# Two states' scan terms added on GpSimd before TensorE turns them

## The chip, the core and the metric

The kernel runs on one core of one Trainium2 chip. It is one program for the whole model of two layers, in float32 throughout (some operands of the attention are float32 rounded for TensorE). The metric is device time in microseconds (us) of the whole program; the times of a kernel are given as the median of several runs, and one further execution is profiled. Engines are named as the profile names them: PE is TensorE's matmul (PEld its weight load), DVE is VectorE, ACT is ScalarE, POOL is GpSimd, SP the queue that issues most DMAs.

## The reference, cut to what matters

The input is 4 images of 128 channels and 64 x 64 places. Layer 0 is a convolution branch with a Mamba scan over the 4096 places of an image; layer 1 is attention over the 4096 places (4 heads of 32) and a mixture of 8 experts, two chosen for each place. The change is inside the scan:

```python
dA = jnp.exp(delta[..., None] * A)
dBu = delta[..., None] * Bm[:, :, None, :] * xin[..., None]

def step(h, inp):
    dA_t, dBu_t, C_t = inp
    h = dA_t * h + dBu_t
    y = jnp.einsum('bdn,bn->bd', h, C_t)
    return (h, y)
...
y = jnp.transpose(ys, (1, 0, 2)) + D_skip * xin
out = y * jax.nn.silu(z) @ out_proj_w.T
```

There are N = 16 states for each of 64 inner channels and each of 4 groups of 32 channels. So y at a place is the sum over 16 states of state times C.

## The kernel before, in words

**Tiling.** An image of 4096 places is cut into NB = 8 blocks of BLK = 512; with 4 images there are 32 blocks. A block's scan has two parts p (two channel groups each, so that 2 x 64 channels fill 128 partitions), and each part has 16 states, taken in pairs. A pair is a *unit* (b, i, p, n) (line 1299): 16 units to a block, 512 in all. A unit takes two *slots* of the main loop (line 1322), an even and an odd one, so a block has 32 slots and the scan has END = 1024.

**A unit's work.** `driven` (799) multiplies the pair's rows of B, fetched by a DMA and the same for all channels, by delta times input into the tile `h` (DVE, 128x1024). `scan` (804) runs the recurrence through both states in one DVE instruction over 1025 elements, with decays `da` that ACT made (`decayed`, 779). In the odd slot `read` (813) multiplies h by the pair's rows of C into `hc`, 128 partitions x 2 states x 512 (DVE, two buffers). `kept` (794) stores the last column of each state for the next block.

**The sum over states** is made on PE: `turned_on` (824) transposes a term of 128x512 in four matmuls of 128x128 that accumulate into one PSUM tile `y`: 16 terms, one for each state, over the 8 units of a part. When a part's last term is in, ACT copies y out as yT, one slot later `turned_back` (839) transposes it back into another tile of the same PSUM pool, and a slot after that `summed_up` (833) lets DVE gate it.

**The order of work** is written out by hand. Every instruction of the main loop goes through `queued` (450), which fixes each engine's order to the order in which the program writes the instructions (so the profile gives one line, L467, for nearly all of them, and tiles tell them apart). In a slot the loop writes: the DMAs for rows to come, the next unit's decays, `driven` (even slot), what is left of a part that was closed, half a step of lane X, the scores and exponentials of one attention group, `scan` (even) or `read` (odd), half a step of lane Y, the terms that are due, the other half of lane Y, the products of the attention group before, the other half of lane X. Lane Y carries the convolutions, norms and inputs of the scan's next blocks; lane X the closing of blocks behind it and the experts. Each lane has one PSUM tile. Norms in both lanes raise a variance to the power -0.5 on POOL (tiles rsX, rsY, 128x4), which ACT (xt) or DVE (tt) then reads.

**When terms are due.** A deque `due` holds (slot, unit, which state, term, whether it ends the part), and the loop takes from its front whatever has come due (lines 1348 to 1359). A unit read in odd slot s has its first term due at s + 1 and its second at s + 2; the first unit of a part has its first term due at s + 3, and as the deque is taken from the front its second follows then too, so that y of the part before has left PSUM.

**Attention** groups (PE scores sc, ACT exponentials pT, PE products av) are ready only when their blocks are closed; they lag behind the scan and run on after its last unit.

Of the kernel before, what the change touches and what calls it, by code (L numbers as in the profile page):

```python
# [24 lines left out]
NST = 16  # L25
# [11 lines left out]
def conv_mamba_attn_moe_kernel(ctx: ExitStack, tc: tile.TileContext, t: dict):  # L37
# [3 lines left out]
    NB = L // BLK  # L41
# [419 lines left out]
    class Queue:  # L461
# [7 lines left out]
    tensor, vector, scalar, gpsimd, sync = (  # L469
        Queue(e) for e in (nc.tensor, nc.vector, nc.scalar, nc.gpsimd, nc.sync)  # L470
    )
# [14 lines left out]
    def flush():  # L486
        for entry in outgoing:
            entry[0] -= 1
            if entry[0] == 0:
                sync.dma_start(out=entry[1], in_=entry[2])  # L490
        outgoing[:] = [entry for entry in outgoing if entry[0]]
# [302 lines left out]
    def kept(unit, h):  # L794
        b, i, p, n = unit
        if i < NB - 1:
            scalar.copy(states[b % 2][:, p, n : n + 2], h[:, :, BLK - 1])

    def driven(unit, h, w):
        b, i, p, n = unit  # L800
        du = in_of[b, i, p][3]
        vector.tensor_mul(h[:, :, 0:BLK], w, du[:, None, :].to_broadcast([P, 2, BLK]))

    def scan(unit, h, da):

        b, i, p, n = unit
        h, da = (a.rearrange("p k q -> p (k q)")[:, 0 : 2 * BLK + 1] for a in (h, da))
        vector.tensor_tensor_scan(
            out=h, data0=da, data1=h, initial=states[b % 2][:, p, n : n + 1],
            op0=ALU.mult, op1=ALU.add,  # L810
        )

    def read(h, w):
        hc = mix.tile([P, 2, BLK], F32, name="hc", bufs=2)
        vector.tensor_mul(hc, w, h[:, :, 0:BLK])
        return hc
# [7 lines left out]
    def turned_on(y, term, first, last):  # L824

        for j in range(NT):
            s = slice(j * P, (j + 1) * P)
            tensor.matmul(
                y[:, s], lhsT=term[:, s], rhs=ident, start=first and j == 0,
                stop=last and j == NT - 1, is_transpose=True,  # L830
            )

    def summed_up(b, i, p, y):
        scanned(b, i, p, y)
        done.add(("scan", b, i, p))
        if p == 1:
            lanes["X"].appendleft((("closed", b, i), closed(b, i), []))

    def turned_back(b, i, p, yT):
        y = ps_y.tile([P, BLK], F32, name="y")  # L840
        for j in range(NT):
            tensor.transpose(y[:, j * P : (j + 1) * P], yT[:, j * P : (j + 1) * P], ident)
        return b, i, p, y
# [184 lines left out]
    def exponentials(group):  # L1028
        pTs = []
        for v, sc in group[3]:  # L1030
            pT = att.tile([P, 2, BLK], F32, name="pT", bufs=4)
            scalar.activation(pT, sc, AF.Exp, scale=ATT_SCALE)
            pTs.append((v, pT))
        return *group[:3], pTs, *group[4:]

    def weighted(group):
        b, q, h, pTs, first, last, prev, final = group
        if first:
            sums[0] = ps_av.tile([P, BLK], F32, name="av")
        av = sums[0]  # L1040
        for k, (v, pT) in enumerate(pTs):
            for u in range(2):
                mm(
                    av[64 * u : 64 * u + 2 * DH, :], v, pT[:, u, :],
                    first and k == 0, last and k == STEP - 1,
                )
        if last:
            avs = att.tile([P, BLK], F32, name="avs", bufs=2)
            if prev is None:
                scalar.copy(avs, av)  # L1050
            else:
                vector.tensor_add(avs, av, prev)


            if not final:
                partial[b, q, h] = dram.tile([P, BLK], F32, name=f"avd{q}{h}")
                send(partial[b, q, h], avs, 3)
                return
            if h == 0:
                total[b, q] = dram.tile([2, 2, NH, DH, BLK], F32, name=f"total{q}")  # L1060
            d = total[b, q]
            send(d[:, :, h].rearrange("u k r q -> (u k) r q"), avs, 3)
            if h == NH - 1:
                work_left = inverted(b, q)
                later.extend((slot + n, work_left) for n in (4, 6, 8))
# [150 lines left out]
    def advance(lane, second):  # L1216

        if inside[lane] != second:
            return False
        while True:  # L1220
            if lane not in running:

                tasks = lanes[lane] if lanes[lane] or slot < END else lanes["X"]
                if tasks and lane == "Y" and tasks[0][0][0] == "closed":
                    return False
                if not tasks or not all(k in done for k in tasks[0][2]):
                    return False

                if (
                    tasks[0][0][0] == "out" and slot < END + 4  # L1230
                    and not 2 <= slot % (2 * NST) < NST + 2
                ):
                    return False
                key, stages, _ = tasks.popleft()
                running[lane] = key, stages(lane) if callable(stages) else stages
            key, stages = running[lane]
            try:
                next(stages)
                inside[lane] = not second
                return True  # L1240
            except StopIteration:
                assert not second
                done.add(key)
                del running[lane]
# [53 lines left out]
    groups = attention_groups()  # L1298
    units = [(b, i, p, n) for b, i in blocks for p in range(2) for n in range(0, NST, 2)]
    END = 2 * len(units)  # L1300

    rows, due, closing, y_of = {}, deque(), deque(), {}
    h_of, slot = {}, 0

    def fetch(*wanted):
        for ahead, k in wanted:
            if ahead < len(units):
                until(("in", *units[ahead][:3]))
                rows[ahead, k] = fetched(units[ahead], k)

    def prepared(ahead, k):
        if ahead < len(units):
            decayed(units[ahead], decays[ahead % 2], k)
            if k:
                h_of[ahead] = carried(units[ahead])

    def ends(unit):
        return unit[3] == NST - 2
# [3 lines left out]
    while (  # L1322
        slot < END or due or closing or summing or waiting or left or later or lanes["X"] or running
    ):
        at, odd = divmod(slot, 2)
        flush()
        if slot == 0:
            fetch((0, 0), (0, 1), (1, 0))
            prepared(0, 0)
            prepared(0, 1)  # L1330
        fetch((at + 2, 0) if odd else (at + 1, 1))
        unit = units[at] if at < len(units) else None
        prepared(at + 1, odd)
        if unit and not odd:
            h = h_of.pop(at)
            driven(unit, h, rows.pop((at, 0)))
        if summing:
            summed_up(*summing)
            summing = None
        advance("X", True)  # L1340
        group = next(groups, None)
        if group:
            group = exponentials(group)
        if unit and not odd:
            scan(unit, h, decays[at % 2])
        if unit and odd:
            hc = read(h, rows.pop((at, 1)))
            late = 2 * (unit[3] == 0)
            due.append((slot + 1 + late, unit, 0, hc[:, 0, :], False))
            due.append((slot + 2, unit, 1, hc[:, 1, :], ends(unit)))  # L1350
        advance("Y", False)
        while closing and closing[0][0] <= slot:
            summing = turned_back(*closing.popleft()[1:])
        while due and due[0][0] <= slot:
            _, (b, i, p, n), k, term, done_with = due.popleft()
            first = n == 0 and k == 0
            if first:
                y_of[b, i, p] = ps_y.tile([P, BLK], F32, name="y")
            turned_on(y_of[b, i, p], term, first, done_with)
            if done_with:  # L1360
                yT = mix.tile([P, BLK], F32, name="yT")
                scalar.copy(yT, y_of.pop((b, i, p)))
                closing.append((slot + 1, b, i, p, yT))
        advance("Y", True)
        if unit and odd:
            kept(unit, h)
        if waiting:
            weighted(waiting)
        waiting = group
        advance("X", False)  # L1370
        while later and later[0][0] <= slot:
            next(later.popleft()[1])
        slot += 1
# [113 lines left out]
```

## Time and profile before

| what | value |
|---|---|
| median of 3 runs | 5234.72 us (5234.31 to 5243.44) |
| the profiled execution | 5221.24 us |
| its span, first to last instruction | 5219.4 us |
| first scan, first scan of the third block (slot 64), last scan start at | 99.4, 307.4, 4605.9 us |
| mean granted TensorE clock | 0.958 |

The page's strip of 40 equal slices shows how the load runs over the span. Each digit is the busy share of a slice in tenths, and PEclk is the granted clock in tenths of full speed:

```profile
PE   4566898999999999899999999999999999999997
PEld 2333444444444444444444444444444444443443
DVE  4888767777788877888788877888788877751332
ACT  3456787788777777688887787788777787756543
POOL 1111101100000000001000000000000001000000
PEclk8677999999999999899999999999999999999998
```

In the first four slices (some 520 us) little attention is ready and PE has gaps; from there to about slice 35 scan, lanes and attention run together; the last four or five slices are attention and experts without a scan. Rows of the page read: line, engine, operation, output tile <- input tiles, shapes, count | busy us of the group, mean ns of one | idle time of the engine before them and what ended most of it. Busy time is a union, so that overlapping matmuls count once, while the mean is the length of one record.

### The profile page before, as it was taken

The numbers are of one execution on the slowest core, as the hardware profiler recorded it, in microseconds if no ns is written. First come the engines' busy times: TensorE is split into PE (matmuls) and PEld (weight loads), VectorE is DVE, ScalarE is ACT, GpSimd is POOL, SyncE is SP. The second block draws the span as 40 slices with busy tenths as digits, with TensorE's granted clock in tenths as the row PEclk, the third lists the DMA queues.
The fourth block names the chain that finished last, engine by engine and source line by source line (L and its number), as shares of the span: only waits on it lengthen the run. The fifth ranks groups of instructions, "written<-read, shape, count | busy, mean of one in ns | idle before, by whom it ended". The sixth has DMA issues, their size and how long they took to land.

```text
span 5219.4 us, 62693 instructions
## 1 busy us (share of the span) xinstructions
PE 4743.5 (91%) x20704; PEld 2300.7 (44%) x20704; DVE 3834.5 (73%) x5809; ACT 3749.8 (72%) x5701; POOL 423.5 (8%) x483
## 2 busy tenths in 40 slices
PE   4566898999999999899999999999999999999997
PEld 2333444444444444444444444444444444443443
DVE  4888767777788877888788877888788877751332
ACT  3456787788777777688887787788777787756543
POOL 1111101100000000001000000000000001000000
PEclk8677999999999999899999999999999999999998
DMA  3556667767776667767766667767766666754542
GB/s 96 188 186 202 206 215 247 232 231 238 244 231 218 227 227 243 238 232 246 260 230 231 224 223 230 262 227 259 259 236 227 215 230 226 263 181 153 184 134 72
DMA packets 451694, 1131.62 MB, mean 217 GB/s; under 512 B 51985, under 2 KB 135330, under 8 KB 451362
## 3 DMA queue, kind: packets, MB, share of 16 engines
q1 hardware_dynamic: 450194, 1126.74, 64.3%
q8 instruction: 166, 2.72, 0.2%
q14 instruction: 166, 1.36, 0.1%
q10 hardware_dynamic: 1168, 0.80, 0.1%
HBM read 967.12 MB, written 143.39 MB: 213 GB/s over the span
## 4 chain that ended last, share of the span: by engine, by line
PE 55%; DVE 18%; ACT 13%; DMA 6%; issue 5%; POOL 2%; SPq 1%; DVEq 0%; ACTq 0%; POOLq 0%
PE av L467 23%; PE sc L467 13%; PE ps_X L467 8%; DVE h L467 6%; PE ps_Y L467 5%; PE y L467 5%; ACT pT L467 4%; ACT L467 3%; DMA ks<-kd 2%; DVE hc L467 2%; ACT xt L467 1%; ACT e L467 1%; DMA rows<-bcd 1%; DVE stX L467 1%; POOL rsX L467 1%
## 5 line engine op out<-in xcount | busy, mean ns | idle before, releaser
L467 ACT ACTIVATE pT<-sc 128x1024 f32<-128x1024 f32 x2048 | 1984.8, 1023 | 940.1 <-PE sc L467 938.4
L467 PE MATMUL av<-pT,v 128*64 128x512 f32 x8192 | 1998.3, 609 | 12.4 <-DVE avs L467 12.4
L467 PE MATMUL sc<-qs,ks 128*128 128x512 f32 x4096 | 1296.1, 436 | 64.4 <-DMA ks<-kd 32.7
L467 DVE TENSOR_TENSOR_SCAN h<-da,state,h 128x1025 f32<-128x1025 f32 x512 | 1204.2, 2352 | 90.0 <-ACT h L467 56.2
L467 PEld LDWEIGHTS sc<-qs,ks 128*128 128x128 f32 x4096 | 701.3, 190 | 793.3 <-ACT pT L467 261.7
L467 PEld LDWEIGHTS av<-pT,v 128*64 128x64 f32 x8192 | 499.5, 137 | 844.4 <-issue 813.8
L467 ACT ACTIVATE da<-delta,amat 128x512 f32<-128x512 f32 x1024 | 743.0, 730 | 1.9
L467 PE MATMUL y<-ident,hc 128*128 128x128 f32 x4096 | 626.6, 284 | 64.9 <-DVE hc L467 64.9
L467 DVE TENSOR_TENSOR hc<-rows,h 128x1024 f32<-128x1024 f32 x512 | 624.2, 1219 | 16.1 <-PE y L467 5.9
L467 DVE TENSOR_TENSOR h<-rows,du 128x1024 f32<-128x1024 f32 x512 | 623.4, 1218 | 14.2 <-DMA rows<-bcd 13.7
L467 PEld LDWEIGHTS y<-ident,hc 128*128 128x128 f32 x4096 | 520.6, 147 | 235.7 <-issue 83.9
L467 ACT ACT_TABLE_LOAD x319 | 409.3, 1283 | 19.5 <-DVE zs L467 14.3
L467 POOL TENSOR_TENSOR rsX<-rsX,mhalf 128x4 f32<-128x4 f32 x92 | 203.8, 2216 | 2524.6 <-DVE rsX L467 2440.5
L467 POOL TENSOR_TENSOR rsY<-rsY,mhalf 128x4 f32<-128x4 f32 x100 | 130.4, 1304 | 2071.0 <-DVE shiftY L467 1560.3
L467 DVE TENSOR_TENSOR avs<-av,prev 128x512 f32<-128x512 f32 x96 | 66.1, 689 | 252.9 <-PE av L467 238.3
L467 PE MATMUL ps_X<-share,w_ew 128*128 128x512 f32 x432 | 215.5, 622 | 8.7 <-DVE share L467 8.5
L467 ACT ACTIVATE xt<-ps_Y,shiftY,rsY 128x128 f32<-128x128 f32 x380 | 143.8, 469 | 106.4 <-POOL shiftY L467 99.0
L467 DVE TENSOR_TENSOR share<-share,xf 128x1024 f32<-128x1024 f32 x128 | 155.9, 1218 | 15.6 <-DMA share<-sharesX 9.9
L467 ACT COPY state<-h 128x2 f32<-128x2 f32 x448 | 88.7, 198 | 93.5 <-DVE h L467 93.5
L467 DVE SCALAR_TENSOR_TENSOR cm<-y,w_fc1w,cm 128x512 f32<-128x512 f32 x192 | 142.8, 744 | 3.4
L467 PE MATMUL ps_Y<-pairs,inxc 128*128 128x512 f32 x256 | 129.2, 629 | 15.6 <-DMA pairs<-xn 10.3
L467 PEld LDWEIGHTS ps_X<-share,w_ew 128*128 128x128 f32 x432 | 73.6, 190 | 146.8 <-issue 98.5
(254 smaller groups left out, 3455.8 us busy)
## 6 DMA issues: line engine op xcount, KB each, us to landing
rows<-bcd SPq DMA_DIRECT2D x1024, 512.0 KB
ks<-kd SPq DMA_DIRECT2D x192, 512.0 KB
qs<-qd SPq DMA_DIRECT2D x161, 512.0 KB
share<-sharesX SPq DMA_DIRECT2D x108, 512.0 KB
v<-vd SPq DMA_DIRECT2D x192, 256.0 KB
ks<-kd SPq DMA_DIRECT2D x128, 256.0 KB
avd<-avs SPq DMA_DIRECT2D x96, 256.0 KB
prev<-avd SPq DMA_DIRECT2D x96, 256.0 KB
```

What stands on the lines that cost most here:

```text
L467: return lambda *args, **kw: queued(op(*args, **kw))
```

## The change

From slot 64 on (ALONE = NB // 2 * NST = 4 x 16) the two terms of a unit are not turned one by one. In the odd slot, straight after `read`, GpSimd adds the second state's half of hc into the first, and PE gets one term of 128x512 to turn in place of two. That term is due at s + 2, or at s + 3 for the first unit of a part, and carries the mark that ends the part. Nothing else is edited.

```diff
@@ -1298,6 +1298,7 @@
     groups = attention_groups()
     units = [(b, i, p, n) for b, i in blocks for p in range(2) for n in range(0, NST, 2)]
     END = 2 * len(units)
+    ALONE = NB // 2 * NST
 
     rows, due, closing, y_of = {}, deque(), deque(), {}
     h_of, slot = {}, 0
@@ -1346,8 +1347,12 @@
         if unit and odd:
             hc = read(h, rows.pop((at, 1)))
             late = 2 * (unit[3] == 0)
-            due.append((slot + 1 + late, unit, 0, hc[:, 0, :], False))
-            due.append((slot + 2, unit, 1, hc[:, 1, :], ends(unit)))
+            if slot < ALONE:
+                due.append((slot + 1 + late, unit, 0, hc[:, 0, :], False))
+                due.append((slot + 2, unit, 1, hc[:, 1, :], ends(unit)))
+            else:
+                gpsimd.tensor_add(hc[:, 0, :], hc[:, 0, :], hc[:, 1, :])
+                due.append((slot + 2 + late // 2, unit, 0, hc[:, 0, :], ends(unit)))
         advance("Y", False)
         while closing and closing[0][0] <= slot:
             summing = turned_back(*closing.popleft()[1:])
```

## The prediction, made before the result was known

> **What bounds the kernel now.** I read the page's table of engines first, then the windows by block, then the chain.
>
> ```profile
> PE 4743.5 (91%) x20704; PEld 2300.7 (44%) x20704; DVE 3834.5 (73%) x5809; ACT 3749.8 (72%) x5701; POOL 423.5 (8%) x483
> ```
>
> PE leads, but a share of the span mixes stages. The windows that follow are five single blocks (16 units each) and the stretch after the last scan; after the length they give busy us of PE, PEld, DVE, ACT and POOL, then the granted clock.
>
> ```profile
> 307.40:426.20 118.80, 75.04 (x282) 41.63 (x281) 98.42 (x126) 63.81 (x120) 13.07 (x13) 0.77 0.55 186
> 551.20:682.50 131.30, 111.23 (x472) 55.47 (x470) 98.52 (x126) 93.99 (x155) 13.06 (x13) 0.91 0.61 205
> ...
> 1401.00:1541.00 140.00, 136.20 (x618) 66.27 (x615) 117.77 (x178) 112.54 (x175) 11.61 (x14) 1.00 0.69 226
> ...
> 1687.00:1830.00 143.00, 128.68 (x578) 64.89 (x576) 118.25 (x178) 108.91 (x174) 11.61 (x14) 0.95 0.69 237
> 1830.00:1974.00 144.00, 140.45 (x630) 68.75 (x627) 117.25 (x176) 115.86 (x180) 11.69 (x15) 0.99 0.69 226
> ...
> 4612.00:5219.40 607.40, 564.22 (x2229) 240.75 (x2228) 168.29 (x464) 300.56 (x334) 12.61 (x13) 0.96 0.41 135
> ```
>
> A regular block (1830 to 1974) takes 9.0 us a unit: PE is busy 97.5% of it (8.8 us a unit), DVE 81% (7.3 us). Where attention has not set in (307 to 426), neither is full. The last 607 us hold no scan and are out of the change's reach. Cut at each scan's start, the same block is uneven:
>
> ```profile
> 1834.60:1847.60 13.00, 13.00 (x54) 5.74 (x52) 6.68 (x7) 11.55 (x17) 0.00 (x0) 1.00 0.89 273
> 1847.60:1862.20 14.60, 14.60 (x78) 7.75 (x77) 9.69 (x19) 14.51 (x21) 1.91 (x1) 1.00 0.35 115
> ...
> 1886.70:1897.00 10.30, 10.30 (x47) 4.89 (x47) 10.23 (x11) 7.58 (x12) 0.00 (x0) 1.00 0.77 259
> ...
> 1964.50:1969.40 4.90, 4.90 (x25) 2.15 (x25) 4.71 (x4) 4.09 (x7) 0.00 (x0) 1.00 0.80 248
> ```
>
> DVE waits for PE in the first two and then has no gap at all. Cut so from 307 us on, DVE is over 90% busy in 226 of 479 stretches. The chain over those scans (307.4 to 4612, 4305 us) says which of the two counts:
>
> ```profile
> by line: PE av L467 22.3%; PE sc L467 12.7%; PE ps_X L467 8.4%; DVE h L467 6.5%; PE y L467 5.9%; ACT pT L467 5.1%; issue 5.0%; PE ps_Y L467 4.1%; ACT L467 3.8%; DMA ks<-kd 2.1%; DVE hc L467 1.9%; ACT xt L467 1.2%; ACT e L467 1.1%; DMA rows<
> ```
>
> So the chain goes from PE to DVE and back; y's transposes are on it for 5.9%, the scan's own DVE work (h and hc) for 8.4%.
>
> **What is removed: transposes on PE.** The rows of the page:
>
> ```profile
> L467 DVE TENSOR_TENSOR_SCAN h<-da,state,h 128x1025 f32<-128x1025 f32 x512 | 1204.2, 2352 | 90.0 <-ACT h L467 56.2
> ...
> L467 PE MATMUL y<-ident,hc 128*128 128x128 f32 x4096 | 626.6, 284 | 64.9 <-DVE hc L467 64.9
> ...
> L467 DVE TENSOR_TENSOR hc<-rows,h 128x1024 f32<-128x1024 f32 x512 | 624.2, 1219 | 16.1 <-PE y L467 5.9
> L467 DVE TENSOR_TENSOR h<-rows,du 128x1024 f32<-128x1024 f32 x512 | 623.4, 1218 | 14.2 <-DMA rows<-bcd 13.7
> ```
>
> The switch is at slot 64, and a block has 32 slots: it takes effect from the third block on, in 480 of 512 units (the instruction order of the built kernel agrees: 2176 such transposes are left and 480 adds stand on POOL). Four transposes a unit go, 1920 in all, at 626.6/4096 = 0.153 us of PE time each (their 284 ns overlap): 294 us of busy PE. Only what is on the chain pays. PE y there is 5.9% of 4305 = 254 us; yT's transposes are 40 us of the 667 us with that name, so hc's part is 239 us, and half of it, **-119 us**, goes. That is the most that this edit can bring while the rest of that chain stays. The first term was due a slot ahead of the second; now both come at the later slot, which already released y and yT, so nothing after it moves. The 65 us that PE waited for hc may shrink with that; it is counted as nothing, since 72 of the 78 hc on the chain are followed there by DVE's next instruction and not by PE.
>
> **What is added: 480 adds of 128x512 on POOL.** No such add is in the trace. The nearest rows are a copy and small products:
>
> ```profile
> 2318.36 0.20 POOL L467 TENSOR_TENSOR shiftY<-shiftY,rsY 128x4 f32<-128x4 f32 x1
> ...
> 2318.58 0.24 POOL L467 COPY y<-y 128x64 f32<-128x64 f32 x1
> ```
>
> A copy of 3 elements takes 0.18 us at 2378.04, so 61 more elements cost 0.06, 1 ns each. Two inputs cost 1 ns an element at the least and 2 if they are read in turn: 0.7 to 1.2 us an add, of which 0.5 to 1.0 reads. I take 1.0 of reading. POOL has room for it (480 x 1.2 = 576 us beside 424). Whether DVE has is the question. A small power on POOL during a scan:
>
> ```profile
> 2452.86 2.35 DVE L467 TENSOR_TENSOR_SCAN h<-da,state,h 128x1025 f32<-128x1025 f32 x1
> 2453.04 2.97 POOL L467 TENSOR_TENSOR rsX<-rsX,mhalf 128x4 f32<-128x4 f32 x1 [74.82 <-DVE rsX L467]
> ```
>
> The same power takes 1.01 us at 2317.27. Here it ends 0.8 us after the scan does (2455.21): it read nothing until DVE was through. In the same way one that came during hc at 2497.86 took 1.98 and got in between hc and the h that follows without a gap. So POOL and DVE exclude each other while DVE reads two inputs from SBUF, and POOL gets its turn at the next change of instruction. No row shows the other direction, since four elements hold nothing up. Bounds per add: 0 if DVE passes, 1.2 us if it waits for the whole add. I take 1.0, because what is exclusive one way is nearest to exclusive both ways.
>
> The Trainium skill, SBUF — State Buffer, "Who interferes with whom", speaks against the change in just this way: a VectorE instruction with two SBUF inputs and a GpSimd instruction that reads SBUF lock each other out, whichever comes first. Its GPSIMD Engine Reference, "Elementwise — side-by-side cycle accounting", gives 4497 ns for an add of 2048 elements, so an estimate of 1.12 us for 512. By these pages each delay would be 1.12 us and not 1.0, and the sum below some 18 us more; by a reading in which ports don't matter it would be 152 us less.
>
> Who is behind the add: on DVE, after 291 of the 480 hc, the next two-input instruction follows at once (most often h), the add gets in after it, and the scan is late by 1.0. In 117 cases up to 1.2 us are free, in 72 more. The delay costs time where DVE ends last:
> - On the chain now: h is 6.5% of 4305 = 280 us, at 1.22 + 2.35 a unit 78 units. 78 x 1.0 = **+78 us**.
> - Of the 226 stretches in which DVE is full, the other 148 are near the chain. With their slack anywhere from 0 to one delay, half is charged: 148 x 0.5 = **+74 us** (0 to 148).
> - In the remaining 254 units the add lies in DVE's wait for PE: nothing. If that wait were gone they would cost 254 us.
> - On POOL, an add keeps the powers issued after it waiting (rsX and rsY; ACT xt and DVE tt wait for them). POOL is 2% of the whole chain, about 104 us, some 50 powers of 2 us; one in ten late by 1.0 is **+5 us** (0 to 50).
> - The clock: PE's load falls from 8.8 to 8.2 of 9.0 us, 91%. The block at 90% (1687 to 1830) had a clock of 0.95, the ones at 97% had 0.99 to 1.00. PE lines named in the chain hold 53% of it, 2280 us; 4% of that would be 91 us if the whole ran slower, but only matmuls behind a gap do: **+15 us** (0 to 91).
>
> No DMA is added or moved, and SP's queue and ACT's instructions stay as they are. Sum: -119 + 78 + 74 + 5 + 15 = +53 us on a span of 5219.4, 5272. The median of the runs is 15.3 us above that span: **5288 us**, 1.0% slower.
>
> **Rivals.**
> - Faster: DVE passes POOL's reads, or its waits for PE (1.7 us a unit in a regular block) take them up. For it: 81% load. Against it: the wait of the power above. Price: -119, with a third given back as the chain goes to ACT and DMA: -80, 5155 us; decided by whether scan and h start later behind an add.
> - DVE becomes the bound: the best block so far, 1401 to 1541, keeps it 84% busy. With 7.35 + 0.8 a unit (0.8: the delays after each hc weighed with the free times above) and no better than 84%, a unit takes 9.7 us, 0.66 more, +317: about 5550 us. It decides if blocks grow beyond 9.5 us. Against it: single stretches with DVE 99% full.
> - Saving and delays cancel within what a measurement of this kernel can tell, 0.2% (10 us): 5235 us.
> - The change does not do all it says: it begins in the third block, not in the middle of the image. The 32 extra units lie where no engine is full; 32 x 1.0 us at most. It is inside the sum.
>
> **How the numbers follow.** Forecast (0.2% to 4% slower) 0.51; faster 0.33; cancelled 0.09; DVE as the bound 0.07. The low end is the faster rival's and some us below it, 5140; the high end charges all 226 full units 1.2 us, all 91 us for the clock and leaves the powers: -119 + 271 + 91 = +243 would be 5478; half of that excess is unlikely to come together, so 5400. The forecast's own range is 5245 to 5400. Slower 0.58, same 0.09, faster 0.33.
>
> **What would show it.** In the profile after: y's matmuls at 2176 and some 330 us busy; a POOL row hc<-hc x480 with a mean well over 1.2 us (it waits in the record); scan, h or share rows with longer means or starts, 0.5 to 1 us a unit; blocks of 9.1 to 9.4 us a unit with PE at 90 to 92% and a clock of 0.95 to 0.98; a chain in which DVE's share rises above 18%. If DVE's rows keep their durations and starts and blocks take 8.7 us, the exclusion one way was all there is, and the prediction is wrong.

## The result and the profile after

The changed kernel takes 5295.49 us (median of 4 runs, 5290.29 to 5299.57) against 5238.53 us before in the same series. The ratio is 1.0109, with a 95% interval of 1.0097 to 1.0121: slower by 57 us. The prediction was 5288 us.

First the page of the changed kernel: its span, its engines, and the groups that answer to those of before, with the new one on POOL.

```profile
span 5292.1 us, 59999 instructions
...
PE 4615.8 (87%) x18784; PEld 2100.0 (40%) x18784; DVE 4119.6 (78%) x5809; ACT 3754.7 (71%) x5701; POOL 1315.9 (25%) x963
...
L467 PE MATMUL av<-pT,v 128*64 128x512 f32 x8192 | 2023.2, 615 | 23.6 <-DVE avs L467 23.2
...
L467 POOL TENSOR_TENSOR hc<-hc 128x512 f32<-128x512 f32 x480 | 823.7, 1716 | 2398.4 <-DVE hc L467 2186.0
L467 DVE TENSOR_TENSOR_SCAN h<-da,state,h 128x1025 f32<-128x1025 f32 x512 | 1337.3, 2612 | 70.5 <-ACT h L467 34.5
...
L467 DVE TENSOR_TENSOR h<-rows,du 128x1024 f32<-128x1024 f32 x512 | 699.8, 1367 | 7.4 <-DMA rows<-bcd 7.4
L467 DVE TENSOR_TENSOR hc<-rows,h 128x1024 f32<-128x1024 f32 x512 | 624.5, 1220 | 25.2 <-DVE h L467 11.9
...
L467 PE MATMUL y<-ident,hc 128*128 128x128 f32 x2176 | 355.9, 293 | 55.0 <-DVE hc L467 36.9
...
L467 DVE SCALAR_TENSOR_TENSOR cm<-y,w_fc1w,cm 128x512 f32<-128x512 f32 x192 | 186.1, 969 | 3.4
```

DVE has the same 5809 instructions and is 285 us busier (3834.5 before). The scan's rows grew by 133 us, h's by 76, the taps' cm (142.8 before) by 43, and the next part's inputs ln and du by 22 and 10; hc itself, which comes ahead of the add, has not changed. So an add lengthened DVE's rows by 285/480 = 0.59 us on average. PE lost 128 us of busy time, less than the 271 that y's rows lost.

Where an add is seen doing this: DVE and POOL of the changed kernel in order of time (start us, us), in a stretch where DVE has no waits. The columns after the engine are line, operation and tiles.

```profile
1997.85 1.22 DVE L467 TENSOR_TENSOR h<-rows,du 128x1024 f32<-128x1024 f32 x1
1999.17 3.19 DVE L467 TENSOR_TENSOR_SCAN h<-da,state,h 128x1025 f32<-128x1025 f32 x1
...
1998.01 2.20 POOL L467 TENSOR_TENSOR hc<-hc 128x512 f32<-128x512 f32 x1 [3.66 <-DVE hc L467]
```

The add is issued when h has just begun (1997.85). Its record ends at 2000.21, 1.14 us after h ends at 1999.07, and beside an idle DVE the whole add takes 1.27 us, as at 2103.44: so it did not get in before h was through. The scan then starts on time, at 1999.17, but takes 3.19 us where it took 2.35. POOL's record covers its wait and DVE's record covers its own, so neither shows an idle gap.

A regular block of the changed kernel, in the window view (length, then busy us of PE, PEld, DVE, ACT, POOL, and the granted clock):

```profile
1857.00:2005.00 148.00, 137.46 (x579) 61.98 (x577) 129.50 (x177) 118.14 (x182) 45.08 (x32) 0.99 0.68 223
```

It takes 9.25 us a unit where it took 9.0. PE is 93% busy in place of 97.5%, and DVE 87.5% in place of 81%. The tail is as long as it was: 611 us from the start of the last scan, 613 before. The chain on the page of after cannot be set beside that of before: its engines' shares add up to 59% of the span only, the rest being unnamed.

### The profile page after: what moved, and what is told of

The parts are those of the page before. It is cut to its first block, busy times and chain, and to the rows that moved or that the text cites. A ratio compares the mean times of both kernels' runs of the same rounds, so it can differ in the third digit from the quotient of the medians.

```text
span 5292.1 us, 59999 instructions
## 1 busy us (share of the span) xinstructions
PE 4615.8 (87%) x18784; PEld 2100.0 (40%) x18784; DVE 4119.6 (78%) x5809; ACT 3754.7 (71%) x5701; POOL 1315.9 (25%) x963
## 4 chain that ended last, share of the span: by engine, by line
PE 28%; DVE 17%; ACT 5%; DMA 4%; issue 4%; POOL 1%; SPq 0%; DVEq 0%; ACTq 0%; POOLq 0%
PE av L467 12%; PE sc L467 7%; DVE h L467 6%; PE ps_X L467 4%; PE ps_Y L467 3%; ACT pT L467 2%; DVE hc L467 2%; DMA ks<-kd 2%; DVE cm L467 1%; PE y L467 1%; DVE share L467 1%; ACT L467 1%; ACT xt L467 1%; DVE stX L467 1%; DVE stY L467 1%
## 5 line engine op out<-in xcount | busy, mean ns | idle before, releaser
L467 PE MATMUL av<-pT,v 128*64 128x512 f32 x8192 | 2023.2, 615 | 23.6 <-DVE avs L467 23.2
L467 PE MATMUL sc<-qs,ks 128*128 128x512 f32 x4096 | 1315.7, 440 | 123.3 <-ACT pT L467 66.0
L467 POOL TENSOR_TENSOR hc<-hc 128x512 f32<-128x512 f32 x480 | 823.7, 1716 | 2398.4 <-DVE hc L467 2186.0
L467 DVE TENSOR_TENSOR_SCAN h<-da,state,h 128x1025 f32<-128x1025 f32 x512 | 1337.3, 2612 | 70.5 <-ACT h L467 34.5
L467 DVE TENSOR_TENSOR h<-rows,du 128x1024 f32<-128x1024 f32 x512 | 699.8, 1367 | 7.4 <-DMA rows<-bcd 7.4
L467 DVE TENSOR_TENSOR hc<-rows,h 128x1024 f32<-128x1024 f32 x512 | 624.5, 1220 | 25.2 <-DVE h L467 11.9
L467 PE MATMUL y<-ident,hc 128*128 128x128 f32 x2176 | 355.9, 293 | 55.0 <-DVE hc L467 36.9
L467 PEld LDWEIGHTS y<-ident,hc 128*128 128x128 f32 x2176 | 292.9, 152 | 168.1 <-issue 61.8
L467 DVE SCALAR_TENSOR_TENSOR cm<-y,w_fc1w,cm 128x512 f32<-128x512 f32 x192 | 186.1, 969 | 3.4
```

The lines of the kernel that those rows point to most:

```text
L467: return lambda *args, **kw: queued(op(*args, **kw))
```

## Experiments

All are set against runs of the kernel before on the same chip. Each edit is shown against the changed kernel unless it says otherwise.

**The add without the saving** (against the kernel before; after the two `due.append`):

```diff
+            if slot >= NB // 2 * NST:
+                spare = mix.tile([P, 496], F32, name="spare")
+                gpsimd.tensor_add(spare, hc[:, 0, 0:496], hc[:, 1, 0:496])
```

> The kernel before with the adds put on POOL beside the old work: from slot 64 on POOL adds 496 of the 512 columns of the two states into a tile that nothing reads, and PE still turns both terms at their old slots, so nothing waits for an add but the reuse of hc two units later. Theory (POOL's reads and DVE's two-input instructions exclude each other, and that is the cost): DVE's rows h, scan, cm and ln grow by about 0.6 us an add (250 to 290 us in all, as in the changed kernel) and the time rises to 5350 to 5420 us. Rival (the cost is the wait of PE for a later term and POOL's queue): no term waits here, so 5230 to 5255 us.

5363.69 us, ratio 1.0239 (1.0213 to 1.0264): 125 us slower than before. No engine's wait in the trace ends with one of these adds, and yet DVE is 268 us busier (4102.2), with rows that grow as in the changed kernel:

```profile
L467 POOL TENSOR_TENSOR spare<-hc 128x496 f32<-128x496 f32 x480 | 814.5, 1697 | 2449.7 <-DVE hc L467 2449.2
L467 DVE TENSOR_TENSOR_SCAN h<-da,state,h 128x1025 f32<-128x1025 f32 x512 | 1331.2, 2600 | 74.3 <-ACT h L467 38.8
```

So the wait of PE for a later term is not the cost. (In the changed kernel PE waits for an add three times, 17.9 us in all.) That it is POOL's reading, and not its being busy, is shown by the fills below.

**The saving without the add:**

```diff
-                gpsimd.tensor_add(hc[:, 0, :], hc[:, 0, :], hc[:, 1, :])
```

> The changed kernel without the add: from slot 64 on the second state's half of hc is left out of y, and PE turns only the first, at the slots of the changed kernel. Theory: this is the saving on PE alone, which I put at 119 us on the chain less what goes to other engines: 5120 to 5190 us, with DVE's rows h and scan at 1.22 and 2.35 us again and DVE busy 3835 us. Rival (with less work PE's granted clock falls and eats the saving): 5200 us or more, with a clock at or below 0.945.

5138.18 us, ratio 0.9805 (0.9784 to 0.9826): 100 us faster. The page's engine line and rows:

```profile
PE 4570.0 (89%) x18784; PEld 2087.9 (41%) x18784; DVE 3833.8 (75%) x5809; ACT 3748.1 (73%) x5701; POOL 423.6 (8%) x483
...
L467 DVE TENSOR_TENSOR_SCAN h<-da,state,h 128x1025 f32<-128x1025 f32 x512 | 1204.5, 2353 | 78.9 <-ACT h L467 44.9
```

DVE's rows are at their old lengths. The clock fell to 0.950 (0.958 before) and the time fell all the same, so the rival's 5200 us did not come. Set beside the changed kernel, the adds cost 5295 - 5138 = 157 us on top of this kernel, and 125 on top of the old one. By the table further down, the extra lies in units 10 to 14 of a block. With PE shorter, DVE has less waiting left there to take a delay up; that this is the reason is likely and not shown.

**POOL as busy, but writing only:**

```diff
-                gpsimd.tensor_add(hc[:, 0, :], hc[:, 0, :], hc[:, 1, :])
+                for _ in range(2):
+                    gpsimd.memset(hc[:, 1, :], 0.0)
```

> As the run without the add (the second state is left out of y), but POOL writes zeros over the second half of hc in two fills of 512 columns, about 1.1 us a unit, in the add's place and with its wait for hc: POOL is as busy and its queue as blocked as with the add, but it reads nothing. Theory (reads exclude): within 15 us of the run without the add, DVE's rows unchanged. Rival (POOL's queue and the powers behind the add cost it): 5270 to 5310 us, as the changed kernel.

5139.20 us, 1 us from the run without the add. The group of the fills and the scan's:

```profile
L467 DVE TENSOR_TENSOR_SCAN h<-da,state,h 128x1025 f32<-128x1025 f32 x512 | 1205.2, 2354 | 79.4 <-ACT h L467 43.9
L467 POOL MEMSET hc<- 128x512 f32 x960 | 515.4, 537 | 2580.2 <-DVE hc L467 2370.5
```

515 us of POOL's time at the add's place, waiting for the same hc, cost nothing. Two fills keep POOL for 1.07 us a unit, an add for 1.26 where nothing holds it up. At that length POOL's queue is not the price, nor are its writes.

**One input in place of two:**

```diff
-                gpsimd.tensor_add(hc[:, 0, :], hc[:, 0, :], hc[:, 1, :])
+                gpsimd.tensor_copy(hc[:, 1, :], hc[:, 0, :])
```

> The changed kernel with a copy on POOL in the add's place: it reads the first half of hc and writes it over the second, which PE no longer turns, so the second state is left out of y. One input of 512 elements is read in place of two. Theory (the pair is held as long as POOL reads, which goes with the number of elements read): DVE's rows grow by about half of the add's 285 us, 100 to 170 us, and the time lies between the run without the add (5138) and the changed kernel (5295): 5165 to 5225 us. Rival (any POOL instruction that reads SBUF holds it for one fixed time): 285 us and 5280 to 5300 us.

5176.92 us, 39 us above the run without the add, and DVE 70 us busier than there (3903.3). The time is inside what was expected, but the rows grew by a quarter of the add's 285 us and not by half (and the time by a quarter too, 39 of 157). Duration of h and of the scan, min/median/max in ns, first for the copy, then for the add:

```profile
L467 DVE TENSOR_TENSOR h<-rows,du x512: 1158/1220/1640, 100.9 to 4563.9; 128x1024 f32<-128x1024 f32 x171
L467 DVE TENSOR_TENSOR_SCAN h<-da,state,h x512: 2337/2354/2650, 102.2 to 4565.4; 128x1025 f32<-128x1025 f32 x171
```

```profile
L467 DVE TENSOR_TENSOR h<-rows,du x512: 1155/1220/2317, 98.6 to 4679.4; 128x1024 f32<-128x1024 f32 x171
L467 DVE TENSOR_TENSOR_SCAN h<-da,state,h x512: 2337/2354/3348, 99.9 to 4680.7; 128x1025 f32<-128x1025 f32 x171
```

At most a copy holds h up for 1640 - 1220 = 0.42 us and an add for 2317 - 1220 = 1.10: 0.8 and 2.1 ns an element, 2.6 times and not twice. POOL's own durations, of the copy and then of the add, go with that:

```profile
L467 POOL COPY hc<-hc x480: 604/1006/2146, 316.5 to 4569.3; 128x512 f32<-128x512 f32 x160
```

```profile
L467 POOL TENSOR_TENSOR hc<-hc x480: 1256/1657/2794, 314.4 to 4685.4; 128x512 f32<-128x512 f32 x160
```

The shortest took 0.60 us for a copy and 1.26 for an add. The longest holds are 0.18 and 0.16 us below these: DVE stands for about as long as POOL's instruction takes by itself. A scan shows some 0.1 us less, as it starts that much after h in any case (1999.07 to 1999.17 above). Why the rows grew four times as much with the add, and not 2.6 times, is open.

**The add on DVE:**

```diff
-                gpsimd.tensor_add(hc[:, 0, :], hc[:, 0, :], hc[:, 1, :])
+                vector.tensor_add(hc[:, 0, :], hc[:, 0, :], hc[:, 1, :])
```

> The changed kernel with the add issued on DVE, straight after hc, in place of POOL. By the rows of its size (128x512, two SBUF inputs) it takes 0.69 us there, 331 us in all, against some 285 us by which POOL's adds lengthened DVE's rows. Theory (DVE's time is what the add costs, on whichever engine it is issued): 5285 to 5330 us, about the changed kernel. Rival (POOL's queue or the wait for it costs the time): DVE has room at 81% load, 5180 to 5240 us.

5285.55 us, ratio 1.0089 (1.0069 to 1.0109), 10 us below the changed kernel. DVE's own adds are 332.2 us (692 ns each) against the 285 us that POOL's cost it. What was moved off PE has to be paid on DVE on either engine, for about the same time.

**Four units of each block.** The kernel before, cut at each scan's start, has stretches in which DVE waits long for PE. With the same number of adds, one run puts them there and one where DVE is full:

```diff
-            if slot < ALONE:
+            if slot < ALONE or at % NST not in (0, 1, 10, 11):
```

> The changed kernel with POOL's add in four units of each block only (the 1st, 2nd, 11th and 12th of 16, from the third block on: 120 adds); every other unit has its two terms turned as before. In the trace of before, DVE stood idle 1.4 and 3.3 us on average in the 1st and 2nd stretch from scan to scan and 1.5 and 2.0 us in the 11th and 12th, with 2.0 to 6.0 us in the stretches behind them, and PE was full there. Theory (an add costs time only where DVE has no wait for PE left to put it in): the saving stays and the delays are absorbed: 120 x 0.21 to 0.46 us off, 5185 to 5220 us. Rival (an add costs its lock wherever it stands): a quarter of the changed kernel's loss, 5245 to 5260 us.

and with `(3, 6, 7, 14)`:

> Four other units of each block take POOL's add, again 120 in all: the 4th, 7th, 8th and 15th, in whose stretches DVE had only 0.4 to 0.8 us of idle time on average in the trace of before. Same number of adds and of transposes saved as in the run with four units (5193). Theory (it is the place that decides): the delays are not absorbed, 5235 to 5275 us, no faster than before. Rival (a few adds are cheap anywhere, and only their number drives the cost): within 12 us of 5193.

The first takes 5192.85 us, ratio 0.9910 (0.9897 to 0.9924), faster than both kernels. The second takes 5285.44 us, ratio 1.0076 (1.0060 to 1.0091). Both have 120 adds and 3616 transposes for y, and 93 us lie between them (88 when each is set against its own runs of before). The scan's and h's rows, first of the faster, then of the slower:

```profile
L467 DVE TENSOR_TENSOR_SCAN h<-da,state,h 128x1025 f32<-128x1025 f32 x512 | 1237.2, 2416 | 88.9 <-ACT h L467 54.5 <-DVE h L467 0.9 <-ACT da L467 0.5
L467 DVE TENSOR_TENSOR h<-rows,du 128x1024 f32<-128x1024 f32 x512 | 631.5, 1233 | 13.8 <-DMA rows<-bcd 9.6 <-ACT zs L467 4.2
```

```profile
L467 DVE TENSOR_TENSOR_SCAN h<-da,state,h 128x1025 f32<-128x1025 f32 x512 | 1236.6, 2415 | 77.2 <-ACT h L467 42.5 <-DVE h L467 0.9 <-ACT da L467 0.5
L467 DVE TENSOR_TENSOR h<-rows,du 128x1024 f32<-128x1024 f32 x512 | 653.3, 1276 | 14.1 <-DMA rows<-bcd 13.8 <-issue 0.2
```

DVE was lengthened in both, by 57 and by 88 us in all (3892.0 and 3922.7 against 3834.5). Those 31 us could explain a third of the 93.

Where in a block the time goes can be counted in the traces, from the start of one unit's scan to the start of the next, in the profiled executions. Changes against the kernel before, in us a block, from the third block on (the run with fills repeats the run without the add to 0.1 us in each column):

| run | units 1 to 3 | 4 to 9 | 10 to 14 | 15, 16 | block |
|---|---|---|---|---|---|
| saving without the add | -1.5 | -0.2 | -1.4 | +0.2 | -2.8 |
| add without the saving | +0.3 | +3.7 | -0.3 | +0.9 | +4.6 |
| changed kernel | -1.3 | +3.6 | -0.9 | +1.0 | +2.4 |
| adds in 1, 2, 11, 12 | -0.8 | -0.1 | -0.3 | +0.1 | -1.0 |
| adds in 4, 7, 8, 15 | -0.6 | +2.5 | -0.3 | +0.4 | +2.0 |

So the saving and its price fall in different places. The saving comes in units 1 to 3 and 10 to 14, in whose stretches DVE stood idle 1.4 to 6.0 us on average before. The price comes mostly in units 4 to 9, with 0.4 to 1.1 us. A rival for the two runs with 120 adds is that one set saves more on PE than the other; but where the saving falls they differ little, and some 2.5 of the 3 us a block between them lie in units 4 to 9. And in units 10 to 14 the changed kernel keeps 0.9 of the 1.4 us saved, though the adds alone cost nothing there.

**Which waits take a delay up.** Four more sets of units:

> As the run with four units, with seven of 16 (1st to 3rd, 10th to 13th: 210 adds), so that it takes in units whose own stretch has less DVE wait in front of the next two-input instruction. Theory: between 5180 and 5230 us, no more than 15 us better than four units since the waits are used up. Rival (lock wherever it stands): 5255 to 5270 us.

> The four units of the faster run (1st, 2nd, 11th, 12th) and the 15th and 16th, 180 adds. In the trace of before DVE runs without a gap through the 15th, 16th and 1st stretch and waits for PE 3.3 and 6.0 us in the 2nd and 3rd, so the delays of all could still go into those waits. Theory in that form (the delay is carried to the next wait): 5165 to 5192 us. Rival (the delay must be absorbed in its own stretch, since PE takes up hc one stretch later): 5200 to 5230 us.

> The run with seven units lost 39 us against the run with four; it added the 3rd, 10th and 13th unit. Here the four get the 10th alone (150 adds). If the 10th carries the loss (in the trace of before 10 of 30 blocks had more than 1 us free behind its hc, and the powers for two norms are issued near it): 5215 to 5235 us. If the 3rd and 13th carry it: 5185 to 5200 us.

> The four units and the 3rd and 13th (180 adds), whose stretches had the longest idle times of DVE in the trace of before (6.0 and 5.2 us on average). If idle time of the own stretch decides: 5170 to 5192 us. If these two carry the loss of the run with seven, because DVE's wait there comes in front of hc and not behind it: 5215 to 5240 us.

| units of 16, counted from 1 | adds | us | ratio (95%) |
|---|---|---|---|
| 1, 2, 11, 12 | 120 | 5192.85 | 0.9910 (0.9897 to 0.9924) |
| and 3, 10, 13 | 210 | 5231.42 | 0.9985 (0.9976 to 0.9994) |
| and 15, 16 | 180 | 5187.77 | 0.9896 (0.9880 to 0.9913) |
| and 10 | 150 | 5197.36 | 0.9920 (0.9906 to 0.9933) |
| and 3, 13 | 180 | 5239.91 | 1.0004 (0.9995 to 1.0014) |

Seven units were a miss for the theory as it stood (at most 15 us better than four and no slower than 5230, and it came out 39 us worse at 5231), and the 3rd and 13th, with the longest idle times of all, carry that loss. So the expectation for idle time in the own stretch (5170 to 5192 us) failed. The order of the 3rd unit's DVE work in the kernel before shows why idle time alone misleads there:

```profile
1847.51 2.35 DVE L467 TENSOR_TENSOR_SCAN h<-da,state,h 128x1025 f32<-128x1025 f32 x1
1854.32 0.69 DVE L467 TENSOR_TENSOR acc<-ps_X,acc 128x512 f32<-128x512 f32 x1 [4.46 <-PE ps_X L467]
...
1856.31 1.22 DVE L467 TENSOR_TENSOR hc<-rows,h 128x1024 f32<-128x1024 f32 x1
1857.45 0.42 DVE L467 TENSOR_SCALAR du<-e 128x512 f32<-128x512 f32 x1
...
1858.70 0.69 DVE L467 TENSOR_TENSOR ln<-ln,du 128x512 f32<-128x512 f32 x1
...
1860.83 1.22 DVE L467 TENSOR_TENSOR h<-rows,du 128x1024 f32<-128x1024 f32 x1
```

The 4.46 us of idle time come in front of hc. Behind it stand the instructions that make the next part's delta and du, and h, without a gap. Over all blocks, 5.6 us of the 6.0 idle us in that unit lie in front of its hc. In the 13th more than half lies behind (3.1 of 5.2 us). The two were not run apart, but the traces tell them apart. The rows of ln, in the faster run with four units and in the run with the 3rd and 13th as well:

```profile
L467 DVE TENSOR_TENSOR ln<-ln,du 128x512 f32<-128x512 f32 x64 | 47.5, 741 | 13.0 <-ACT ln L467 7.4
```

```profile
L467 DVE TENSOR_TENSOR ln<-ln,du 128x512 f32<-128x512 f32 x64 | 66.2, 1035 | 12.4 <-ACT ln L467 6.8
```

All 30 adds of the 3rd unit hold up ln or the du ahead of it, 27 us in all, and that unit's stretch is 27 us longer over the 30 blocks. Behind the 13th unit's adds, scan and h are no more than 1.5 us longer in all than with four units, and its own stretch 3 us longer over the blocks. So the 3rd carries most of the loss. Some 11 us of it come up in the 6th unit; how they get there is open. The sets do not add up exactly: the seven units take 8 us less than the six with the 3rd and 13th. The 15th and 16th have little idle time of their own and cost nothing: their two stretches grow by 0.5 us a block against the run with four units, and units 1 to 3 are 0.9 us shorter, so their delays are carried into the waits that follow. Their gain over four units is not clear of the intervals.

## Why the prediction was right

The sum was +53 us on the span, and +57 us was measured on the medians. The mechanism was right; that the number came so close is in part luck. The saving was 19 us smaller than forecast, and the two small terms, 20 us together, were not seen as such: the errors cancel. What the runs show is -100 for the saving and +157 for the adds. By its steps:

- **The saving, -119 us on the chain.** Shown, and somewhat smaller: 100 us without the add. Half of hc's part of the chain came near it; by the table above nearly all of the saving falls in units 1 to 3 and 10 to 14. The other figure given, 294 us of busy PE, was mis-sized: PE's busy time fell by 173 us (4743.5 to 4570.0). Of the row's 627 us, other matmuls overlap 197. The time that y's transposes of hc fill alone fell by 197 us (429 to 232), and all other matmuls grew by 23, sc's row by 13 and av's by 6 among them.
- **POOL and DVE exclude each other in both directions.** Only one direction stood in the trace of before, and the other was taken as its mirror. Shown: scan, h, cm and ln lengthen behind an add, and writes alone do nothing. An add was taken to hold for 1.0 us; the longest seen is 1.10. The 291 units said to have an instruction right behind hc would make 291 us at 1.0, and DVE grew by 285.
- **The price, +78 and +74 us.** The sum of both terms, 152, lies between the 125 and 157 us that the adds cost on the old kernel and on the one with the saving. Counting full stretches at half price was a guess that held as a sum; the two terms were not measured apart. That the price is paid where DVE is nearly full is shown by the table. That adds in the remaining units are free is too simple. The runs by units show that a delay is taken up only by a wait that comes behind it.
- **The powers behind the add on POOL, +5 us.** Not seen: 1 us between the fills and no add, though a fill leaves POOL sooner than an add that has to wait. ACT's wait for shiftY behind these powers rose from 99 to 140 us in the changed kernel, but also to 127 with the add on DVE, so POOL's queue is not what lengthens it in the main.
- **The clock, +15 us.** This step was wrong in its reading. A block with PE at 93% kept 0.99, where 0.95 was expected near 91%; the blocks on either side of it, with PE at 84% and 78%, had 0.92 and 0.88 (0.95 and 0.88 before, at 90% and 85%). The mean fell from 0.958 to 0.945, and to 0.950 in the run that was 100 us faster. What the clock cost is open; no run held it fixed.

Of the rivals, the faster one named as its test whether scan and h start later behind an add. The scan shown starts on time and ends late, so it is the duration that decides, and it speaks against that rival. DVE did not become the bound in the sense of the next rival: it went past the 84% taken as its ceiling, to 87.5% in a regular block, and blocks stayed at 9.25 us a unit.

## What to carry to other kernels

An add moved to GpSimd is not off VectorE's books: while it reads, VectorE's instructions with two SBUF inputs stood still here, and 128x512 on GpSimd cost VectorE 0.59 us on average against 0.69 for doing the add itself. Before moving work, price both halves apart, one kernel with the saving alone and one with the cost alone, and see in which stretches of the loop each falls: here they fell in different ones. Where the saving is real and the cost is a delay, put the work where a wait comes after it (idle time in front of it does not help): 120 adds so placed made this kernel 0.9% faster, and 480 of them everywhere made it 1.1% slower.

## What was not expected of the hardware

A two-input add on POOL held DVE 2.6 times as long as a one-input copy of the same length (1.10 and 0.42 us for 512 elements), where twice was expected from twice the elements read; the holds follow what the two take on POOL alone, 1.26 and 0.60 us. And the wait does not show as idle time: DVE's busy time rose by 285 us without one instruction more, so a row's maximum against its median tells of such a hold where the idle columns don't.
